# Two graph-attention layers on one core: three row-sum counts per sample instead of six, and five projections issued in halves

## The chip, the cores and the metric

The kernel runs on one core of a Trainium2 chip. The metric is the device time of one execution in microseconds (us). Before the change it is 3097.54 us, the median of three runs (3097.45 to 3101.15).

The engines named below are those of the profile: PE does the matrix multiplications (PEld is its weight load), DVE, ACT and POOL are the vector, scalar and general engines, and SP issues transfers (DMAs). Each engine works through its own queue in the order in which the program was written.

## The reference

Sixteen samples of 1024 nodes with 256 features go through two attention layers. What is computed, cut to what matters:

```
for layer in (0, 1):                      # 4 heads of 64, then 8 heads of 32
    h = relu(layernorm(x))                # per node
    q, k, v = h Wq, h Wk, h Wv            # layer 1 adds biases
    s = q k^T / sqrt(D), -inf where adj == 0
    x = x + (softmax(s) v) Wo + bo        # softmax over the 1024 keys
```

All of it is in float32. The softmax needs two things of each masked and exponentiated score tile p (keys on the partitions, queries along the row): the product with v, and the sum over the keys by which the product is divided.

## The kernel before, in words

**Steps.** The work of a layer on one sample is cut into groups: two halves of 512 queries (`qh`), and in each half two groups of heads (`g`). A group of layer 1 has four heads and eight steps; step j takes the 128 keys of tile j against 512 queries for all four heads. A group of layer 0 has four steps. A layer-0 sample is 16 steps, a layer-1 sample 32. The stream runs layer 0 of sample 0 and then, for b = 0, 1, ..., layer 0 of sample b+1 and layer 1 of sample b. In this document c is the first step of layer 1 of a sample b; its four groups start at c, c+8, c+16 and c+24, and c+32 begins the next layer-0 stage. A *pair* is an even step and the odd one behind it.

**What a step does.** `scores` (line 459) makes four products of 128 by 512, in two PSUM tiles of two banks each. `exponentials` lets DVE mask each tile into SBUF (line 482, two instructions) and ACT take the exponential in place (line 488). Two steps later, `weigh` (line 500) multiplies the exponentials with v. POOL then adds the odd step's tiles to the even step's (line 613).

**PSUM.** All tiles of two banks come from one pool with three buffers, handed out in turn (`psum_pair`): two for the scores of each step, and one for every projection (`kq` and `values`: q, k and v of another sample or layer) or output product (`end_half`). So without a projection the scores of the next step take the buffer that is left over and the first of this step; with one in between they take both buffers of this step, and must wait until DVE has read them.

**Where a projection goes.** The stream of `Stream.run` is written out by hand: `later(i, f)` puts f at step i. Functions in `LARGE` (k, q, values, end_half) are issued at the end of their step. If an even layer-1 step has one, its `weigh` is put off to the odd step, which then does two. PE's order in such a pair is: scores, projection, scores, weigh, weigh. In a pair without one it is scores, weigh, scores, weigh.

**The sums over keys.** `count` (line 351) multiplies exponentials with a matrix of ones. In layer 1 a tile is first added up on the way: POOL adds odd to even steps, and `accumulate` (line 597) is a DMA from POOL's queue that adds one even step's tile of 1 MB to another's. For groups 0 to 2 of a sample the tiles of steps 0 to 3 are added into one and counted, and those of steps 4 to 7 into another and counted: six counts in a sample, of which five are issued in two halves of 256 columns, in steps of their own (`halves`), and one whole (512 columns). Each is put at a fixed number of steps after its tile (`waits`). The last group has one count. After the count come `spread`, `invert`, `fetch` and `normalize`, at steps after the group's end that the tuple `at` gives. The sample before the last and the last sample have orders of their own for some groups (`brief`, `pairs`).

**The projections of the next layer-0 sample.** While layer 1 of sample b runs, `block_inputs` puts the k, q and v products of sample b+2's layer 0 into its steps: for the first half of the nodes at c+8 (k), c+16 (q) and c+18 (v), for the second at c+22 (k), c+26 (q) and c+30 (v). There are fourteen such samples (b = 0 to 13).

The exponentials' tiles of even steps have seven buffers, those of odd steps two (for each half): DVE in step j+4 writes where POOL's addition of step j read.

Of the kernel before, what the change touches and what calls it, by code (L numbers as in the profile page):

```python
# [18 lines left out]
P = 128  # L19
# [71 lines left out]
def fast_program(ctx, tc, a, w, loads, chk):  # L91
# [89 lines left out]
    class Inputs:  # L181
# [76 lines left out]

        def kq(self, half, is_q):
            if half == 0 and not is_q:  # L260
                self.kT = actp.tile([P, 2, N], F32, tag="kT", name=f"kT_{self.n}")
                self.v = actp.tile([P, NT, E], F32, tag="v", name=f"v_{self.n}")
            if is_q:
                to = self.qT[half] = actp.tile(
                    [P, 2, 512], F32, tag="qT", bufs=3, name=f"qT_{self.n}_{half}"
                )
            else:
                to = self.kT[:, :, ts(half, 512)]
            wt = w.q if is_q else w.k
            pq = psum_pair(f"pq_{self.n}_{half}_{int(is_q)}")  # L270
            for m in range(2):
                for c in range(2):
                    nc.tensor.matmul(  # L273
                        pq[:, m, :], wt[self.layer][:, c, ts(m, P)], self.hT[half][:, c, :],
                        start=(c == 0), stop=(c == 1),
                    )
            if self.layer == 0:
                if is_q:
                    nc.vector.tensor_copy(to, pq)
                else:  # L280
                    nc.scalar.copy(to, pq)
            else:
                for m in range(2):
# [14 lines left out]

        def k(self, half):
            self.kq(half, False)  # L300

        def q(self, half):
            self.kq(half, True)

        def values(self, half):
            pv = psum_pair(f"pv_{self.n}_{half}").rearrange("p a (t e) -> p (a t) e", e=E)
            for i in range(4):
                for c in range(2):
# [3 lines left out]
                    )  # L312
            nc.scalar.copy(self.v[:, ts(half, 4), :], pv)

# [4 lines left out]
    class Group:  # L319


        def __init__(self, inp, mask, qh, g, half):
# [10 lines left out]

            self.waits = ((5, 5), (7, 7), (7, 6), None)[2 * qh + g]

# [190 lines left out]
    class Stream:  # L526
# [72 lines left out]
        def count_steps(self, i, st):  # L599
# [7 lines left out]
            elif j % 2:  # L607
# [8 lines left out]
                elif gr.pairs:  # L616
                    self.halves(i + 3, gr, one, j == 1, False)
                elif j == 1:
                    gr.one = one
                elif j == 3:  # L620
                    self.accumulate(one, gr.one)
                    gr.one = one
                    if not gr.last:
                        self.halves(i + gr.waits[0], gr, one, True, False)
                    if gr.brief:
                        self.later(i + 6, gr.count, one, True, False)
                elif gr.brief and j == 5:
                    self.halves(i + 5, gr, one, False, False)
                elif gr.brief:
                    self.later(i + 4, gr.count, one, False, st.last)  # L630
                elif j == 5:
                    gr.two = one
# [21 lines left out]
        def end_group(self, i, gr):  # L654
# [121 lines left out]
    def block_inputs(inp, half, turn, put, place, *at):  # L776
# [4 lines left out]
        for i, f in zip(at, (inp.k, inp.q, inp.values)):  # L781
            later(i, f, half)

# [18 lines left out]
    for b in range(B - 1):  # L802
# [14 lines left out]
        if b + 2 < B:  # L817
# [3 lines left out]
            if b == 0:  # L821
                norms(other, 0, a + 12, a + 14, c, c + 1, bias=c + 34)
                block_inputs(other, 0, c + 2, c + 3, c + 4, c + 8, c + 16, c + 18)
                norms(other, 1, c + 3, c + 4, c + 6, c + 7, bias=c + 36)
                block_inputs(other, 1, c + 8, c + 9, c + 12, c + 22, c + 26, c + 30)
# [267 lines left out]
```

## Time and profile before

| | |
|---|---|
| median of three runs | 3097.54 us |
| the profiled execution's own time | 3100.21 us |
| its span, first to last instruction | 3098.4 us |
| PE busy | 3072.7 us, 99% of the span |
| DVE busy | 2484.3 us, 80% |
| POOL busy | 2352.5 us, 76% |
| ACT busy | 2233.5 us, 72% |
| accumulating DMAs (line 597) | 133, 7.8 us each from issue to landing, 920 ns of POOL for each issue |
| layer-1 stage of sample 5 (1151.43 to 1264.48 us) | 113.05 us: PE 113.02, DVE 94.80, POOL 94.60, ACT 82.83 busy |

The page's first part gives each engine's busy time and its share of the span. PE is busy nearly all the time, so time is gained or lost where PE gets less or more to do, or where it is made to wait. The samples repeat almost exactly: the distance from the layer-1 stage's start to the next layer-0 stage is 113.05 to 114.06 us in samples 1 to 13. So the steps of one sample, read from the timeline, stand for the others.

### The profile page before, as it was taken

What the parts mean: (1) busy time and instruction counts of PE and PEld (TensorE: products, weight loads), DVE (VectorE), ACT (ScalarE), POOL (GpSimd) and SP (SyncE); (2) the same over time, 40 slices, a digit from 0 to 9 for tenths busy, and PEclk for the clock granted to TensorE, in tenths of its full rate; (3) what the DMA queues carried; (4) which work ended last, traced back from release to release, by engine and by line L of the source; (5) the groups of instructions that cost most, each with busy time, mean ns of one, the idle gap of its engine ahead of it and who ended that gap; (6) DMA issues with size and microseconds to landing.
All of it is one profiled execution on the core that took longest, in us unless ns stands there. A gap on an engine that the chain in (4) does not pass through costs nothing.

```text
span 3098.4 us, 47101 instructions
## 1 busy us (share of the span) xinstructions
PE 3072.7 (99%) x17404; PEld 1221.5 (39%) x17404; DVE 2484.3 (80%) x2754; ACT 2233.5 (72%) x2440; POOL 2352.5 (76%) x1358
## 2 busy tenths in 40 slices
PE   9999999999999999999999999999999999999998
PEld 4443433434334343343434334343343433434332
DVE  5778788887878888788887888878788787887776
ACT  6677777777777777777777777777777777776775
POOL 3568778687887868778687786877868788786886
PEclk9999999999999999999999999999999999999999
DMA  4225546454453544635445463554545545453331
GB/s 129 59 64 118 127 105 130 121 109 119 108 136 111 117 118 104 143 108 117 121 102 135 107 129 106 114 130 106 127 115 111 127 109 122 118 114 85 76 77 33
DMA packets 259230, 341.38 MB, mean 110 GB/s; under 512 B 58288, under 2 KB 218288, under 8 KB 241968
## 3 DMA queue, kind: packets, MB, share of 16 engines
q0 software_dynamic: 19152, 139.47, 22.9%
q1 hardware_dynamic: 239840, 198.82, 22.7%
q8 instruction: 139, 2.28, 0.3%
q14 instruction: 99, 0.81, 0.1%
HBM read 149.95 MB, written 47.96 MB: 64 GB/s over the span
## 4 chain that ended last, share of the span: by engine, by line
PE 93%; DMA 2%; DVE 2%; ACT 1%; SPq 1%; POOL 1%; issue 1%; DVEq 0%; ACTq 0%; POOLq 0%
PE ps L459 31%; PE po L500 29%; PE pq L273 14%; PE pv L309 8%; PE py L441 7%; PE pz L351 4%; DMA turned<-hn 1%; DVE p L482 1%; POOL p L613 1%; SPq L152 0%; ACT p L488 0%; DMA inv<-vd 0%; DMA p<-p 0%; DMA sums<-s 0%; ACT hn L217 0%
## 5 line engine op out<-in xcount | busy, mean ns | idle before, releaser
L482 DVE SCALAR_TENSOR_TENSOR p<-mask,ps 128x1024 f32<-128x1024 fp8e5 x1536 | 1792.7, 1215 | 352.2 <-PE ps L459 337.2
L488 ACT ACTIVATE p<-p 128x1024 f32<-128x1024 f32 x1536 | 1607.2, 1056 | 630.9 <-DVE p L482 574.6
L613 POOL TENSOR_TENSOR p<-p,p 128x1024 f32<-128x1024 f32 x510 | 1212.5, 2428 | 170.7 <-PE po L500 170.7
L459 PE MATMUL ps<-qT,kT 32*128 32x512 f32 (+1 forms) x6144 | 1070.1, 628 | 4.5 <-DVE p L482 2.6
L500 PE MATMUL po<-p,v 128*32 128x512 f32 (+1 forms) x6144 | 980.9, 600 | 2.6 <-ACT cat L363 2.2
L459 PEld LDWEIGHTS ps<-qT,kT 32*128 32x128 f32 (+1 forms) x6144 | 348.9, 184 | 586.6 <-issue 248.5
L500 PEld LDWEIGHTS po<-p,v 128*32 128x32 f32 (+1 forms) x6144 | 234.5, 118 | 683.0 <-issue 480.9
L513 POOL TENSOR_TENSOR p<-p 128x1024 f32<-128x1024 f32 x128 | 302.4, 2363 | 134.8 <-DVE p L512 129.4
L512 POOL TENSOR_TENSOR p<-p,p 128x1024 f32<-128x1024 f32 x64 | 150.8, 2356 | 204.3 <-DVE p L509 188.3
L411 POOL TENSOR_TENSOR cat<-cat,inv 128x512 f32<-128x512 f32 x127 | 175.7, 1390 | 94.0 <-DMA inv<-vd 93.8
L309 PE MATMUL pv<-wv,hT 128*128 128x256 f32 x1024 | 237.8, 385 | 0.0
L441 PE MATMUL py<-wo,cat 128*128 128x256 f32 x1008 | 236.0, 387 | 1.5 <-POOL cat L411 1.5
L273 PE MATMUL pq<-hT,wq 128*128 128x512 f32 x512 | 236.6, 605 | 0.1
L273 PE MATMUL pq<-hT,wk 128*128 128x512 f32 x512 | 236.6, 605 | 0.1
L309 PEld LDWEIGHTS pv<-wv,hT 128*128 128x128 f32 x1024 | 189.4, 190 | 72.5 <-DVE p L482 21.4
L441 PEld LDWEIGHTS py<-wo,cat 128*128 128x128 f32 x1008 | 187.1, 191 | 76.7 <-issue 25.1
L351 PE MATMUL pz<-p,ones 128*32 128x256 f32 (+1 forms) x1928 | 181.3, 445 | 0.9 <-DMA p<-p 0.9
L509 DVE TENSOR_TENSOR p<-p 128x1024 f32<-128x1024 f32 x128 | 179.8, 1405 | 0.0
L597 POOL DMA_DIRECT2D p<-p x133 | 122.4, 920 | 63.3 <-POOL p L613 30.6
L217 ACT ACTIVATE hn<-x,shift,rstd 128x256 f32<-128x256 f32 x256 | 138.2, 588 | 43.6 <-DMA turned<-hn 29.3
L446 DVE TENSOR_TENSOR x<-py,x 128x1024 f32<-128x1024 f32 x63 | 77.1, 1224 | 102.0 <-PE py L441 101.3
L363 ACT COPY cat<-po 128x512 f32<-128x512 f32 x128 | 73.3, 573 | 116.6 <-PE py L441 96.5
(52 smaller groups left out, 1702.6 us busy)
## 6 DMA issues: line engine op xcount, KB each, us to landing
p<-p POOLq DMA_DIRECT2D x133, 1024.0 KB, 7.8
adj<-in_adj_dram SPq DMA_DIRECT2D x512, 128.0 KB, 3.1
turned<-hn SPq DMA_DIRECT2D x58, 512.0 KB, 3.8
hT<-turned SPq DMA_DIRECT2D x232, 128.0 KB, 2.9
x<-in_x_dram SPq DMA_DIRECT2D x128, 128.0 KB, 3.1
inv<-vd SPq DMA_DIRECT2D x128, 128.0 KB, 3.0
inv<-vd SPq DMA_DIRECT2D x252, 64.0 KB, 3.5
out_dram<-x SPq DMA_DIRECT2D x124, 128.0 KB, 2.2
```

The lines of the kernel that those rows point to most:

```text
L273: nc.tensor.matmul(pq[:, m, :], wt[self.layer][:, c, ts(m, P)], self.hT[half][:, c, :], start=(c == 0), stop=(c == 1),)
L309: nc.tensor.matmul(pv[:, i, :], self.hT[half][:, c, ts(i, P)], w.v[self.layer][:, c, :], start=(c == 0), stop=(c == 1),)
L351: nc.tensor.matmul(self.s[ts(r, 32), q], w.ones.to_broadcast([P, 32]), of[:, q], start=start and not part, stop=stop and part != 0,)
L411: nc.gpsimd.tensor_mul(o, o, inv)
L441: nc.tensor.matmul(py[:, i, :], self.half.cat[:, c, ts(i, P)], w.o[self.layer][:, c, :], start=(c == 0), stop=(c == 1),)
L459: nc.tensor.matmul(st.ps[i // 2][:, i % 2, :], gr.inp.kT[r * D : (r + 1) * D, gr.g, ts(kt, P)], gr.inp.qT[gr.qh][r * D : (r + 1) * D, gr.g ...
L482: nc.vector.scalar_tensor_tensor(out=half, in0=gr.mask.m[gr.qh][:, kt // 4, :, kt % 4].unsqueeze(1).to_broadcast([P, 2, 512]), scalar=-EDG ...
L488: nc.scalar.activation(half, half, AF.Exp, scale=gr.scale)
L500: nc.tensor.matmul(gr.o[r * D : (r + 1) * D, :], gr.inp.v[:, kt, h * D : (h + 1) * D], st.halves[i // 2][:, i % 2, :], start=(kt == 0), st ...
L509: nc.vector.tensor_add(a, a, b)
L513: nc.gpsimd.tensor_add(a, a, b)
L613: nc.gpsimd.tensor_add(half, half, of)
```

## The change

Groups 0, 1 and 2 of a layer-1 sample get one count instead of two. The tile of steps 0 and 1 is added by DMA to that of steps 2 and 3 as before; that one is now added to the tile of steps 4 and 5, and that to the tile of steps 6 and 7, two steps later. The three DMAs follow each other, since each reads what the one before wrote. The last tile is counted whole (512 columns), nine steps after the group's last addition (eight for the third group), and `spread` and `invert` move back to match; `normalize` and `end_half` keep their steps.

`k`, `q` and `values` take an argument `part`. With it they issue only one half of the products, into a PSUM tile of their own, and copy out only that half. Five of the six projections of sample b+2 are issued in this way, each half in an even step: k at c+8 and c+10, q at c+14 and c+16, and for the second half of the nodes k at c+20 and c+22, q at c+24 and c+26, v at c+28 and c+30. The first half's v stays whole at c+18.

```diff
-        def kq(self, half, is_q):
+        def kq(self, half, is_q, part=None):
...
-            pq = psum_pair(f"pq_{self.n}_{half}_{int(is_q)}")
-            for m in range(2):
+            pq = psum_pair(f"pq_{self.n}_{half}_{int(is_q)}_{part}")
+            parts = slice(0, 2) if part is None else slice(part, part + 1)
+            for m in range(2)[parts]:
...
             if self.layer == 0:
                 if is_q:
-                    nc.vector.tensor_copy(to, pq)
+                    nc.vector.tensor_copy(to[:, parts], pq[:, parts])
                 else:
-                    nc.scalar.copy(to, pq)
+                    nc.scalar.copy(to[:, parts], pq[:, parts])
...
-        def values(self, half):
-            pv = psum_pair(f"pv_{self.n}_{half}").rearrange("p a (t e) -> p (a t) e", e=E)
-            for i in range(4):
+        def values(self, half, part=None):
+            pv = psum_pair(f"pv_{self.n}_{half}_{part}").rearrange("p a (t e) -> p (a t) e", e=E)
+            tiles = slice(0, 4) if part is None else slice(2 * part, 2 * part + 2)
+            for i in range(4)[tiles]:
...
-            nc.scalar.copy(self.v[:, ts(half, 4), :], pv)
+            nc.scalar.copy(self.v[:, ts(half, 4), :][:, tiles], pv[:, tiles])
...
-            self.waits = ((5, 5), (7, 7), (7, 6), None)[2 * qh + g]
+            self.waits = (9, 9, 8, 4)[2 * qh + g]
...
-                elif j == 3:
-                    self.accumulate(one, gr.one)
-                    gr.one = one
-                    if not gr.last:
-                        self.halves(i + gr.waits[0], gr, one, True, False)
...
-                elif not gr.last:
-                    self.accumulate(one, gr.two)
-                    if gr.qh:
-                        self.later(i + 6, gr.count, one, False, True)
-                    else:
-                        self.halves(i + gr.waits[1], gr, one, False, True)
-                else:
-                    self.later(i + 1, self.accumulate, one, gr.two)
-                    self.later(i + 4, gr.count, one, True, True)
+                elif gr.last and j == 5:
+                    gr.two = one
+                elif not st.last:
+                    self.accumulate(one, gr.one)
+                    gr.one = one
+                else:
+                    of, k = (gr.two, 1) if gr.last else (gr.one, 2)
+                    self.later(i + k, self.accumulate, one, of)
+                    self.later(i + gr.waits, gr.count, one, True, True)
...
-                at = ((6, 12, 15, 19), (8, 12, 14, 17, 19), (6, 9, 11, 14), None)[2 * gr.qh + gr.g]
+                at = ((10, 13, 15, 19), (10, 14, 15, 18, 19), (8, 11, 12, 14), None)[2 * gr.qh + gr.g]
...
         for i, f in zip(at, (inp.k, inp.q, inp.values)):
-            later(i, f, half)
+            if type(i) is tuple:
+                for part in range(2):
+                    later(i[part], f, half, part)
+            else:
+                later(i, f, half)
...
-                block_inputs(other, 0, c, c + 1, c + 2, c + 8, c + 16, c + 18)
+                block_inputs(other, 0, c, c + 1, c + 2, (c + 8, c + 10), (c + 14, c + 16), c + 18)
...
-                block_inputs(other, 1, c + 7, c + 8, c + 12, c + 22, c + 26, c + 30)
+                block_inputs(other, 1, c + 7, c + 8, c + 12, (c + 20, c + 22), (c + 24, c + 26), (c + 28, c + 30))
```

More of the change, by code (lines that the diff above doesn't have):

```diff
@@ L257, in place_blocks @@
                 )
-        def kq(self, half, is_q):
-            if half == 0 and not is_q:
+        def kq(self, half, is_q, part=None):
+            if half == 0 and not is_q and not part:
                 self.kT = actp.tile([P, 2, N], F32, tag="kT", name=f"kT_{self.n}")
@@ L263, in kq @@
             if is_q:
-                to = self.qT[half] = actp.tile(
-                    [P, 2, 512], F32, tag="qT", bufs=3, name=f"qT_{self.n}_{half}"
-                )
+                if not part:
+                    self.qT[half] = actp.tile(
+                        [P, 2, 512], F32, tag="qT", bufs=3, name=f"qT_{self.n}_{half}"
+                    )
+                to = self.qT[half]
             else:
@@ L278, in kq @@
                 if is_q:
-                    nc.vector.tensor_copy(to, pq)
+                    nc.vector.tensor_copy(to[:, parts], pq[:, parts])
                 else:
-                    nc.scalar.copy(to, pq)
+                    nc.scalar.copy(to[:, parts], pq[:, parts])
             else:
-                for m in range(2):
+                for m in range(2)[parts]:
                     if is_q:
@@ L297, in test, with k, q @@
                 )
[L299 to L303, printed above, removed]
-        def values(self, half):
-            pv = psum_pair(f"pv_{self.n}_{half}").rearrange("p a (t e) -> p (a t) e", e=E)
-            for i in range(4):
+        def k(self, half, part=None):
+            self.kq(half, False, part)
+        def q(self, half, part=None):
+            self.kq(half, True, part)
+        def values(self, half, part=None):
+            pv = psum_pair(f"pv_{self.n}_{half}_{part}").rearrange("p a (t e) -> p (a t) e", e=E)
+            tiles = slice(0, 4) if part is None else slice(2 * part, 2 * part + 2)
+            for i in range(4)[tiles]:
                 for c in range(2):
@@ L619, in count_steps @@
                     gr.one = one
-                elif j == 3:
+                elif gr.brief:
+                    if j == 3:
+                        self.accumulate(one, gr.one)
+                        self.later(i + 6, gr.count, one, True, False)
+                    elif j == 5:
+                        self.halves(i + 5, gr, one, False, False)
+                    else:
+                        self.later(i + 4, gr.count, one, False, True)
+                elif gr.last and j == 5:
+                    gr.two = one
+                elif not st.last:
                     self.accumulate(one, gr.one)
                     gr.one = one
-                    if not gr.last:
-                        self.halves(i + gr.waits[0], gr, one, True, False)
[L625 to L632, printed above, removed]
-                elif not gr.last:
-                    self.accumulate(one, gr.two)
-                    if gr.qh:
-                        self.later(i + 6, gr.count, one, False, True)
-                    else:
-                        self.halves(i + gr.waits[1], gr, one, False, True)
-                else:
-                    self.later(i + 1, self.accumulate, one, gr.two)
-                    self.later(i + 4, gr.count, one, True, True)
+                else:
+                    of, k = (gr.two, 1) if gr.last else (gr.one, 2)
+                    self.later(i + k, self.accumulate, one, of)
+                    self.later(i + gr.waits, gr.count, one, True, True)
         def halves(self, i, gr, one, start, stop):
@@ L822, in fast_program @@
                 norms(other, 0, a + 12, a + 14, c, c + 1, bias=c + 34)
[L823 removed]
+                block_inputs(other, 0, c + 2, c + 3, c + 4, (c + 8, c + 10), (c + 14, c + 16), c + 18)
                 norms(other, 1, c + 3, c + 4, c + 6, c + 7, bias=c + 36)
[L825 removed]
+                block_inputs(other, 1, c + 8, c + 9, c + 12, (c + 20, c + 22), (c + 24, c + 26), (c + 28, c + 30))
             else:
                 norms(other, 0, a + 10, a + 12, a + 13, a + 15, bias=c + 34)
[L828 removed]
+                block_inputs(other, 0, c, c + 1, c + 2, (c + 8, c + 10), (c + 14, c + 16), c + 18)
                 norms(other, 1, c + 2, c + 4, c + 5, c + 6, bias=c + 36)
[L830 removed]
+                block_inputs(other, 1, c + 7, c + 8, c + 12, (c + 20, c + 22), (c + 24, c + 26), (c + 28, c + 30))
             at = 5, 8, 10, 12, 14, 45, 49, 51, 53
```

## The prediction

> **What bounds the kernel now.** First the page: engines and the chain that ended last.
>
> ```profile
> PE 3072.7 (99%) x17404; PEld 1221.5 (39%) x17404; DVE 2484.3 (80%) x2754; ACT 2233.5 (72%) x2440; POOL 2352.5 (76%) x1358
> ...
> PE 93%; DMA 2%; DVE 2%; ACT 1%; SPq 1%; POOL 1%; issue 1%; DVEq 0%; ACTq 0%; POOLq 0%
> ```
>
> PE is never idle for long and carries the chain. Second, the groups with the shapes apart: the counts and DVE's masking.
>
> ```profile
> L351 PE MATMUL pz<-p,ones 128*32 128x256 f32 x1360 | 107.0, 380 | 0.9 <-DMA p<-p 0.9
> L351 PE MATMUL pz<-p,ones 128*32 128x512 f32 x568 | 75.0, 600 | 0.0
> L597 POOL DMA_DIRECT2D p<-p x133 | 122.4, 920 | 63.3 <-POOL p L613 30.6 <-PE po L500 17.3 <-DMA p<-p 12.2
> ```
>
> By these rows fewer counts look like pure gain. Whether they are shows only in the order of time: PE's timeline in sample 5 (start, length, line), from step c+13 (1202.21).
>
> ```profile
> 1202.21 1.14 PE L459 MATMUL ps<-qT,kT 32*128 32x512 f32 x8
> 1203.28 1.92 PE L500 MATMUL po<-p,v 128*32 128x512 f32 x16
> 1205.14 1.14 PE L459 MATMUL ps<-qT,kT 32*128 32x512 f32 x8
> 1206.21 1.07 PE L500 MATMUL po<-p,v 128*32 128x512 f32 x8
> 1207.09 0.61 PE L351 MATMUL pz<-p,ones 128*32 128x256 f32 x8
> 1207.64 1.14 PE L459 MATMUL ps<-qT,kT 32*128 32x512 f32 x8
> ...
> 1210.13 1.15 PE L459 MATMUL ps<-qT,kT 32*128 32x512 f32 x8
> 1211.29 3.70 PE L273 MATMUL pq<-hT,wq 128*128 128x512 f32 x8
> 1214.92 0.71 PE L459 MATMUL ps<-qT,kT 32*128 32x512 f32 x4
> ```
>
> DVE's timeline beside it, and its place at step c+8, whose scores start at 1184.70:
>
> ```profile
> 1206.31 2.35 DVE L482 SCALAR_TENSOR_TENSOR p<-mask,ps 128x1024 f32<-128x1024 fp8e5 x2 [0.51 <-PE ps L459]
> 1208.88 4.78 DVE L482 SCALAR_TENSOR_TENSOR p<-mask,ps 128x1024 f32<-128x1024 fp8e5 x4 [0.22 <-PE ps L459]
> ...
> 1185.47 1.24 DVE L243 STREAM_TRANSPOSE hn<-hn 128x1024 f32<-128x1024 f32 x1
> 1186.63 2.31 DVE L482 SCALAR_TENSOR_TENSOR p<-mask,ps 128x1024 f32<-128x1024 fp8e5 x2
> ```
>
> Read three things. A step with half a count lasts 2.50 us (1205.14 to 1207.64), and DVE's two maskings take 2.39 of it. From the start of the scores DVE needs 1.17 us to begin and is done with both tiles at 1208.66, 3.52 to 3.53 us after. A whole projection puts the odd step's scores 4.79 us behind the even step's (1210.13 to 1214.92): 1.16 of scores, 3.63 of products. So today they never meet a tile that DVE still reads. Where they do, in sample 14, the trace shows what happens:
>
> ```profile
> 2886.53 1.13 PE L459 MATMUL ps<-qT,kT 32*128 32x512 f32 x4
> 2886.91 6.81 DVE L482 SCALAR_TENSOR_TENSOR p<-mask,ps 128x1024 f32<-128x1024 fp8e5 x6
> 2888.12 1.13 PE L459 MATMUL ps<-qT,kT 32*128 32x512 f32 x4 [0.47 <-DVE p L482]
> 2889.18 1.07 PE L500 MATMUL po<-p,v 128*32 128x512 f32 x8
> ```
>
> The first tile's products run, the second tile's wait for the end of a masking, and the step's weigh starts 1.06 us after they begin, so the whole delay passes on.
>
> **The change part by part. Counts.** A sample loses ten half counts and one whole, and gains three whole ones. By PE's rows a half adds 0.43 us to a step (2.50 against 2.07 us for a bare step of sample 14, 2884.46 to 2886.53), a whole one 0.86 behind weighs (step c+31 lasts 3.78 against 2.92) or 1.00 between scores and a projection (c+4 lasts 5.72, c+2 4.72). But the steps with half counts are at another limit: the next step's second tile needs the buffer whose masking ends 2.46 us after the scores' start, so a removed half gives back 0.04 of its 0.43. That gain must come from filling the room with the halved projections.
>
> **Halved projections.** The same products in twice as many tiles. A half is 1.8 to 1.9 us of PE, so the odd step's scores could start 3.0 us after the even step's. They take the two buffers of those scores, as the projection has the third; the second is free at 3.53. Then come 1.06 us to the weighs and 1.86 us of two weighs (1203.28 to 1205.14): a pair lasts 3.53 + 1.06 + 1.86 = 6.45 us, where PE alone would need 3.0 + 2.92 = 5.92. Behind the waiting scores stand both weighs and the next scores on PE; DVE, ACT and POOL wait for these.
>
> Now the twelve pairs from c+8 to c+30. Before, by the starts of the scores: 7.63, 5.08, 7.73, 5.00, 7.71, 7.65, 5.00, 7.71, 5.00, 7.71, 5.00, 8.58, together 79.8 us (1184.70 to 1264.48). After:
> - c+10, 14, 16, 20, 22, 28, 30: 6.45 each.
> - c+8: DVE comes late from the transposition at c+7 and ends 4.24 us after the scores (1186.63 + 2.31 - 1184.70): 4.24 + 2.92 = 7.16.
> - c+12, an output product: 7.73 as before. c+18: 7.65 + 1.00 for the first group's count = 8.65. c+26: count and half projection, 1.07 + 1.0 + 1.9 + 2.92 = 6.9; the count covers the wait.
> - After c+16: DVE does statistics until 4.76 us after the scores, then the q copy (0.61, half of the 1224 ns row, to 0.75, the row of the same size with a bias; I take 0.65), so its next masking ends at 6.6 and c+18 loses 0.15.
> - After c+22: transposition and statistics end at 5.88 in the trace, the reciprocal moved here (0.25) makes it 6.1, the next masking ends at 7.25 and the one behind at 8.4. The scores of c+24 wait until 7.25, its own maskings run from 8.4 to 10.7, and the pair ends at 10.7 + 2.92 = 13.6 instead of 12.9: c+24 counts 7.19.
>
> Together 82.9 us: +3.1. The third group's count lands at c+33, in layer 0, where PE is the limit: +0.86. So +4.0 us a sample; fourteen samples: +56 us. Sample 14 has the new counts without halves; its POOL-bound pair at c+14 (13.19 us) may gain or lose. I take 0, between -3 and +4.
>
> **The rest, costed at nothing.** 45 more accumulating DMAs are 45 x 0.92 = 41 us of POOL, which has 94.6 of 113 us of work in the stage; a pair with one is 4.72 + 0.92 = 5.64 of 6.45. The second DMA of a group waits for the first: issued a pair apart, with 7.8 us from issue to landing, it holds POOL's queue 1.35 us, and the statistics' small operations and the next additions stand behind it. DVE wants the second half of an odd tile some 0.7 us after POOL frees it. In the first group the pair is 7.63 long; in the second the pair behind is c+18, with its whole v; in the third c+26 has the count. I take 0; the other end is DVE 1.5 us late in two groups of each sample, +42. Each count stands at least three pairs behind its last DMA's issue, and all seven even buffers come free before reuse. ACT gets three copies in halves (2 x 0.57 for 1.01), DVE two: 0.1 us each, in idle time. On SP the four small DMAs of `spread` move to c+19, c+27 and c+33; behind the last stands a mask load that is used a layer-0 pair (9 us) later and lands in 3.1, so that is free.
>
> The profiled execution took 3100.2 us, so this sum gives 3156; against the median of the runs, 2.7 lower, 3154.
>
> **Two rules beside the trace.** The Trainium skill (Perfetto Trace Analysis, section Optimization Strategy) says that the same gap repeating on the engine that should be saturated can mean too little PSUM for the next tile. The 0.47 us row above is such a gap, and a projection in halves asks for one more tile each; by this rule the sum is the one above, and by PE's work alone it would be 3065. The same skill (DMA: Bandwidth & Descriptors, section Anatomy of one DMA — SWDGE (gpsimd) path) fits a POOL-issued DMA with 2.0 us + bytes / 436e3, which is an estimated 4.4 us for 1 MB; the trace has 7.8, and goes into the sum. By the page no DMA would wait for another.
>
> **The rivals.** *The fill works (ends on the other side).* If DVE freed the second tile by 3.0 us, nine pairs would last 5.92, and 53.3 + 7.73 + 8.65 + 6.9 = 76.6, +0.86 = -2.4 us a sample: 3065. For it: PE sat idle only 1.3 us in all of the run for DVE's masking before the layer-1 scores (the scores' row by shape). Against: the 3.53 repeats at nearly every step. It decides where half a projection takes more than 2.4 us or masking ends 0.5 us sooner. *The late maskings are absorbed:* without the three extra terms (0.7, 0.15, 0.74), +2.4 a sample: 3131. *POOL becomes the wait:* DVE stands behind additions held by the serial DMA, +42: 3196; the point is POOL starting a pair's additions over 0.7 us behind the weighs. For it: in sample 14 POOL already held DVE for 1.66 us at 2909.26. *The counts do not pay at all* is part of the forecast.
>
> **How the numbers follow.** Forecast 0.62, absorbed 0.12, POOL 0.14, fill works 0.08; 0.04 for something between fill and absorbed. 0.2% of the time is 6 us, about what a measurement tells from no change. Slower: 0.62 + 0.12 + 0.14 + 0.02 = 0.90, same 0.02, faster 0.08. The range leaves out the fill, the cases between, and some of the POOL case: 3128 to 3195.
>
> **What would show it.** In the timeline after, pairs with half a projection last 6.4 to 6.5 us from scores to scores; in the odd step the second tile's products begin 3.53 us after the even step's scores, on the end of a masking, so that these scores' merged row lengthens from 1.14 to some 1.6 us. PE's idle time hardly grows by the page, since the first tile's products fill most of the wait: the loss shows in the pairs, not in the share. Masking still follows the scores by 1.17 us. Wrong if those pairs last 5.9, if POOL's additions appear as DVE's releaser in most samples, or if the layer-0 stages lengthen by more than the count.

## The result, and the profile after

The changed kernel takes 3198.16 us, the median of four runs (3192.42 to 3200.18); the kernel before, on the same chip, 3098.58. The ratio is 1.032 (95% interval 1.0305 to 1.0331): slower by about 100 us, where 56 had been forecast. The direction held, and so did the reason for the part that lies in layer 1; the time lies 3 us above the range. Below, the numbers behind a time are its ratio to the kernel before, run beside it, and the 95% interval. Each time is the median of the executions in the faster of two states; one execution of experiment 8, 3495.73 us at a granted clock of 0.849 where the others have 0.994 to 0.996, is left out.

The page after, engines, then the row of POOL's issues of the accumulating DMAs.

```profile
PE 3139.8 (98%) x16444; PEld 1228.5 (38%) x16444; DVE 2522.4 (79%) x2782; ACT 2249.1 (70%) x2482; POOL 2387.7 (75%) x1403
```

```profile
L601 POOL DMA_DIRECT2D p<-p x178 | 163.2, 917 | 136.2 <-DMA p<-p 102.4
```

The groups with the shapes apart, of the changed kernel: layer 1's scores and the counts (columns: count of instructions, busy us, mean ns, idle time before them and what ended it).

```profile
L463 PE MATMUL ps<-qT,kT 32*128 32x512 f32 x4096 | 682.1, 641 | 6.4 <-DVE p L486 3.3 <-ACT kT L290 1.6
L355 PE MATMUL pz<-p,ones 128*32 128x512 f32 x808 | 106.9, 601 | 0.0
L355 PE MATMUL pz<-p,ones 128*32 128x256 f32 x160 | 12.4, 381 | 0.0
```

The work did get less: the counts take 119.3 us where they took 182.0. Yet PE is "busy" 67 us longer. Layer 1's scores alone went from 592.3 to 682.1 us with the same 4096 instructions and nearly the same mean (640 and 641 ns). A step's scores are two tiles side by side; where the second waits, the first covers it, and the page books the wait as busy time. PE's timeline of sample 5 shows it, from c+14 (1238.28):

```profile
1238.28 1.14 PE L463 MATMUL ps<-qT,kT 32*128 32x512 f32 x8
1239.35 1.98 PE L276 MATMUL pq<-hT,wq 128*128 128x512 f32 x4
1241.26 1.72 PE L463 MATMUL ps<-qT,kT 32*128 32x512 f32 x8
1242.91 1.92 PE L504 MATMUL po<-p,v 128*32 128x512 f32 x16
1244.77 1.14 PE L463 MATMUL ps<-qT,kT 32*128 32x512 f32 x8
```

DVE's timeline beside it:

```profile
1239.45 2.35 DVE L486 SCALAR_TENSOR_TENSOR p<-mask,ps 128x1024 f32<-128x1024 fp8e5 x2 [0.50 <-PE ps L463]
1241.72 0.68 DVE L282 COPY qT<-pq 128x512 f32<-128x512 f32 x1
```

The odd step's scores begin 2.98 us after the even step's and last 1.72 us instead of 1.14, because their second tile waits for DVE, which is done with the even step's second tile only at 1241.80 (1239.45 + 2.35), 3.52 us after its scores. The pair lasts 6.49 us (1238.28 to 1244.77); 6.45 was forecast, 5.92 is PE's work.

From the first to the last scores the run got 97.1 us longer (3049.3 to 3146.4, by the starts of the scores). They come from these places, to the rounding:

| place | before | after | forecast of the difference |
|---|---|---|---|
| layer-1 pairs of fourteen samples | 113.30 a sample | 116.51, together +44.9 | +44 (14 x 3.15) |
| c+32, the third group's count | 9.12 | 9.98, together +12.0 | +12 |
| c+40, a layer-0 pair | 11.05 | 13.16, together +29.5 | 0 |
| the other layer-0 pairs | 56.36 | 56.57, together +3.0 | 0 |
| sample 14's layer 1 | 114.00 | 114.72, +0.7 | 0 (-3 to +4) |
| the last sample | 100.78 | 107.79, +7.0 | 0 |

So the layer-1 stage costs what the forecast said. What was missed lies outside it, above all at c+40. The timelines of SP, DVE and PE in sample 5 around it (c+36 starts at 1320.70, c+40 at 1339.91), after:

```profile
1334.51 2.49 SPq L152 DMA_DIRECT2D adj<-in_adj_dram  x4
1337.05 2.54 SPq L407 DMA_DIRECT2D inv<-vd  x4
1339.69 2.66 SPq L388 DMA_DIRECT2D sums<-s  x4
```

```profile
1344.01 0.25 DVE L396 RECIPROCAL vn<-sums 128x16 f32<-128x16 f32 x1 [3.65 <-DMA sums<-s]
1344.18 4.55 DVE L486 SCALAR_TENSOR_TENSOR p<-mask,ps 128x1024 f32<-128x1024 fp8e5 x4
```

```profile
1345.39 1.56 PE L463 MATMUL ps<-qT,kT 64*128 64x512 f32 x4 [2.64 <-DVE p L486]
1346.88 4.87 PE L504 MATMUL po<-p,v 128*64 128x512 f32 x16
```

and the same place of SP and PE before (c+36 starts at 1284.45, c+40 at 1303.66):

```profile
1287.59 2.24 SPq L403 DMA_DIRECT2D inv<-vd  x4
1298.20 2.76 SPq L152 DMA_DIRECT2D adj<-in_adj_dram  x4
1301.07 3.01 SPq L384 DMA_DIRECT2D sums<-s  x4
```

```profile
1306.74 1.13 PE L459 MATMUL ps<-qT,kT 64*128 64x512 f32 x4 [0.23 <-DVE p L482]
1307.80 3.65 PE L500 MATMUL po<-p,v 128*64 128x512 f32 x16
```

The third group's `fetch` (four DMAs, 2.54 us of SP) stood at c+36 before the change and stands at c+37 now: the third entry of its tuple `at` went from 11 to 12. The last group's `spread` is at c+37 as well, and so is a mask load (line 152), which SP issues 13.8 us after the scores of c+36 in both kernels. Before, the fetch went out ahead of that load, and SP then stood until 1298.20 in any case. Now the fetch has to wait behind the load, between it and the four small DMAs with the last group's sums. These are issued 19.0 us after the scores of c+36 instead of 16.6; DVE's reciprocal stands 3.65 us at the head of DVE's queue waiting for them, and four maskings stand behind it. PE waits 2.64 us where it waited 0.23. Then comes something more: the weigh behind the wait takes 4.87 us, not 3.65. The table by stretches of the changed kernel (stretch; its length and PE's busy time, PEld, DVE, ACT and POOL; then PE's granted clock, DMA share, GB/s) says why:

```profile
1346.00:1348.00 2.00, 2.00 (x8) 0.50 (x6) 2.00 (x3) 1.86 (x3) 0.19 (x1) 0.50 0.74 277
1348.00:1350.00 2.00, 2.00 (x9) 0.53 (x8) 1.97 (x4) 1.86 (x3) 0.00 (x0) 0.66 0.78 212
1350.00:1352.00 2.00, 2.00 (x11) 0.59 (x8) 1.48 (x2) 1.11 (x2) 0.31 (x1) 1.00 0.71 201
```

After the gap the granted clock falls to half for some three microseconds. The pair went from 11.37 to 15.43 us: 2.41 of waiting, 0.43 and 1.22 of the same products at half rate. Samples 3 to 6 had this (14.7 to 15.4 us); nine others took 12.5 to 12.7 us (10.9 to 11.9 before), and sample 13 lost nothing.

The row for that reciprocal sums the waits over the run: 38.3 us now against 15.4 before.

```profile
L396 DVE RECIPROCAL vn<-sums 128x16 f32<-128x16 f32 x95 | 22.9, 241 | 38.3 <-DMA sums<-s 37.9
```

### The profile page after: what moved, and what is told of

Same layout as the page of the kernel before. It is cut to its first block, busy times and chain, and to the rows that moved or that the text cites. A ratio compares the mean times of both kernels' runs of the same rounds, so it can differ in the third digit from the quotient of the medians.

```text
span 3196.3 us, 45453 instructions
## 1 busy us (share of the span) xinstructions
PE 3139.8 (98%) x16444; PEld 1228.5 (38%) x16444; DVE 2522.4 (79%) x2782; ACT 2249.1 (70%) x2482; POOL 2387.7 (75%) x1403
## 5 line engine op out<-in xcount | busy, mean ns | idle before, releaser
L617 POOL TENSOR_TENSOR p<-p,p 128x1024 f32<-128x1024 f32 x510 | 1215.3, 2449 | 171.1 <-PE po L504 166.3
L463 PE MATMUL ps<-qT,kT 32*128 32x512 f32 (+1 forms) x6144 | 1165.7, 630 | 31.1 <-DVE p L486 25.1
L463 PEld LDWEIGHTS ps<-qT,kT 32*128 32x128 f32 (+1 forms) x6144 | 388.1, 184 | 721.1 <-DVE p L486 307.4
L516 POOL TENSOR_TENSOR p<-p,p 128x1024 f32<-128x1024 f32 x64 | 150.8, 2356 | 184.0 <-DVE p L513 169.0
L601 POOL DMA_DIRECT2D p<-p x178 | 163.2, 917 | 136.2 <-DMA p<-p 102.4
L513 DVE TENSOR_TENSOR p<-p 128x1024 f32<-128x1024 f32 x128 | 215.1, 1681 | 0.4 <-issue 0.2
L313 PE MATMUL pv_None<-wv,hT 128*128 128x256 f32 x800 | 185.7, 385 | 0.0
L313 PEld LDWEIGHTS pv_None<-wv,hT 128*128 128x128 f32 x800 | 148.0, 190 | 57.2 <-issue 34.1
L167 ACT ACTIVATE mask<-adj,numbers 128x1024 fp8e5<-128x1024 int32 x128 | 145.7, 1140 | 30.9 <-DMA adj<-in_adj_dram 30.9
L217 ACT ACTIVATE hn<-x,shift,rstd 128x256 f32<-128x256 f32 x256 | 138.1, 588 | 29.1 <-DMA turned<-hn 18.3
L226 POOL TENSOR_TENSOR x<-x,bo 128x1024 f32<-128x1024 f32 x64 | 156.8, 2522 | 0.0
L519 POOL TENSOR_TENSOR p<-p,p 128x1024 f32<-128x1024 f32 x64 | 151.7, 2370 | 5.0
L178 ACT ACTIVATE mask<-mask,numbers 128x1024 fp8e5<-128x1024 fp8e5 x128 | 144.1, 1136 | 0.0
```

Source lines behind the costliest of these rows:

```text
L226: nc.gpsimd.tensor_add(rows, rows, w.bo[self.layer].unsqueeze(1).to_broadcast([P, 4, E]))
L313: nc.tensor.matmul(pv[:, i, :], self.hT[half][:, c, ts(i, P)], w.v[self.layer][:, c, :], start=(c == 0), stop=(c == 1),)
L463: nc.tensor.matmul(st.ps[i // 2][:, i % 2, :], gr.inp.kT[r * D : (r + 1) * D, gr.g, ts(kt, P)], gr.inp.qT[gr.qh][r * D : (r + 1) * D, gr.g ...
L513: nc.vector.tensor_add(a, a, b)
L601: nc.gpsimd.dma_start(one, two, accum_op=ALU.add)
L617: nc.gpsimd.tensor_add(half, half, of)
```

## The experiments

All kernels here compute the whole reference; they differ in order, buffers and the way of the sums alone.

**1. The counts alone**, with all projections whole at their old steps.

```diff
-                block_inputs(other, 0, c, c + 1, c + 2, (c + 8, c + 10), (c + 14, c + 16), c + 18)
+                block_inputs(other, 0, c, c + 1, c + 2, c + 8, c + 16, c + 18)
...
-                block_inputs(other, 1, c + 7, c + 8, c + 12, (c + 20, c + 22), (c + 24, c + 26), (c + 28, c + 30))
+                block_inputs(other, 1, c + 7, c + 8, c + 12, c + 22, c + 26, c + 30)
```

> The changed kernel with whole projections at their old steps, so only the counts and the serial DMAs are changed. Theory A (two losses: in layer 1 the halved projections make the odd step's scores wait for PSUM buffers, about 45 us; in layer 0 a late transfer of the last group's sums holds DVE, about 30 us of the 45 there): the layer-1 stage falls below that of before, since pairs that lost their half counts go from 5.00 to 4.5 us as in sample 14 (five pairs, -2.5), and whole counts at c+18 and c+26 cost 1.0 each and the one at c+30 goes (-0.9): -1.4 us a sample; the layer-0 stages keep all of their +3.2 us a sample and the end its +8 us: about 3098 - 19 + 45 + 8 = 3131. Rival B (the serial DMAs hold POOL and POOL holds DVE in layer 1): the layer-1 stages stay 3 us longer than before and the time stays near 3198.

Measured: 3179.89 us, 1.0262 (1.0245 to 1.0279), between the two expectations. The layer-0 stages are 3.25 us longer, as the expectation had it (c+40 is late here too, 12.85), and the last sample 5.3 (8 was expected). The bare pairs came out at 4.50 as expected as well. The miss is the rest of layer 1, which is 1.8 us a sample longer where 1.4 shorter was expected: c+12 lasts 9.35 us, not 7.7, c+24 5.53, not 4.5, and c+16, c+22 and c+30 7.9, some 0.2 more than expected. For c+12 the timelines show the POOL rival of the prediction at work. In sample 5, POOL at the second DMA of the group, then DVE and PE at c+12:

```profile
1216.24 0.88 POOL L601 DMA_DIRECT2D p<-p  x1 [1.05 <-DMA p<-p]
1216.85 2.83 POOL L415 TENSOR_TENSOR cat<-cat,inv 128x512 f32<-128x512 f32 x2
1219.35 7.32 POOL L617 TENSOR_TENSOR p<-p,p 128x1024 f32<-128x1024 f32 x3
```

```profile
1224.38 3.48 DVE L486 SCALAR_TENSOR_TENSOR p<-mask,ps 128x1024 f32<-128x1024 fp8e5 x3 [0.96 <-POOL p L617]
```

```profile
1225.65 3.72 PE L445 MATMUL py<-wo,cat 128*128 128x256 f32 x16 [1.06 <-DVE p L486]
```

POOL stands 1.05 us for the first DMA before it can issue the second; normalisation and additions follow late, DVE's masking waits 0.96 us for an addition, PE's output product 1.06 us for a buffer that DVE holds. So without the halves POOL does become the wait; with them the pairs are long enough (6.49 us) that c+12 lasts 7.84.

**2. The halves alone**, with the counts, their DMAs and the times of the kernel before.

```diff
-            self.waits = (9, 9, 8, 4)[2 * qh + g]
+            self.waits = ((5, 5), (7, 7), (7, 6), None)[2 * qh + g]
...
-                at = ((10, 13, 15, 19), (10, 14, 15, 18, 19), (8, 11, 12, 14), None)[2 * gr.qh + gr.g]
+                at = ((6, 12, 15, 19), (8, 12, 14, 17, 19), (6, 9, 11, 14), None)[2 * gr.qh + gr.g]
```

Between the two places `count_steps` has its old branches back.

> The kernel before with its counts, and only the five projections in halves at the new steps. Theory A: pairs without a count 6.5 us (the wait for the buffers), pairs that keep their half counts about 6.9 us (the half count between scores and projection covers the wait, and costs its own time), c+8 7.2, c+30 7.4; together 84.2 us for the twelve pairs against 79.8: +4.4 us a sample in layer 1, nothing in layer 0: about 3160. The DMA transfers and POOL's queue are those of before, so rival B (the serial DMAs) expects about 3098, or less.

Measured: 3161.40 us, 1.0203 (1.0186 to 1.022), as the theory of the buffers had it. Pairs with half a projection last 6.49, with a half count beside it 6.93; layer 1 takes 117.88 us a sample against 113.30, layer 0 is unchanged (76.56 against 76.53), and so is the last sample (100.78). The halves alone cost 62 us, all in layer 1; the counts alone 81; both together 100, not 143. The difference lies in layer 1, where the halves alone cost 4.6 us a sample, the counts alone 1.8 and both together 3.2: the longer pairs hide waits that the counts alone bring, c+12 above all.

**3. The fetch a step later.** The changed kernel with one number changed: the third group's `fetch` goes behind the last group's sums in SP's queue.

```diff
-                at = ((10, 13, 15, 19), (10, 14, 15, 18, 19), (8, 11, 12, 14), None)[2 * gr.qh + gr.g]
+                at = ((10, 13, 15, 19), (10, 14, 15, 18, 19), (8, 11, 13, 14), None)[2 * gr.qh + gr.g]
```

> The changed kernel with one number moved: the third group's fetch one step later (12 to 13), so that its four DMAs stand behind the last group's four sums DMAs in SP's queue and not ahead of them. Theory A: the sums land 2 us earlier, DVE's reciprocal at c+39 waits 0.5 us as before instead of 2.6 to 3.2, the layer-0 pair at c+40 goes back from 13.2 (mean) to about 11.0 us: 14 x 2.1 = 29 us less, about 3169. Rival C (a third more bytes of accumulating DMA slow the small transfers): the pair keeps its length, 3198.

Measured: 3170.31 us, 1.0226 (1.0209 to 1.0243): 28 us of the 100 hang on this one place in a queue. (The fetch at its old step c+36, with the later `invert`, was not run.) c+40 goes from 13.16 to 10.94. In sample 5 the sums are now issued first, and the reciprocal waits 0.76 us:

```profile
1327.04 2.90 SPq L388 DMA_DIRECT2D sums<-s  x4
...
1336.24 1.82 SPq L407 DMA_DIRECT2D inv<-vd  x4
```

```profile
1331.11 0.26 DVE L396 RECIPROCAL vn<-sums 128x16 f32<-128x16 f32 x1 [0.76 <-DMA sums<-s]
```

**4. The weigh between.** Even steps with half a projection keep their weigh, so that PE does scores, weigh, half projection, scores, weigh, and the odd step's scores begin later.

```diff
-                f.__name__ in LARGE for f, _ in self.due.get(i, [])
+                f.__name__ in LARGE and len(args) < 2 for f, args in self.due.get(i, [])
```

> The changed kernel, but an even step with half a projection keeps its own weigh between its scores and the half projection (PE: scores, weigh, half, scores, weigh). All work, buffers and DMAs are the same, only PE's order differs. Theory A: the odd step's scores come 3.9 us after the even step's, when both tiles have been read (3.53): the pairs at c+10, 14, 16, 20, 28 and 30 go from 6.49 to 6.0 us, c+8 from 7.2 to 6.3, c+22 and c+24 together lose 0.4: 4.0 us a sample, about 3198 - 56 = 3142. If the half pairs are held by DVE, ACT or POOL instead, they keep 6.49 us and the time 3198.

Measured: 3209.69 us, 1.0362 (1.0344 to 1.0379): a miss. PE's timeline, sample 5, c+14 to c+17:

```profile
1244.70 1.98 PE L276 MATMUL pq<-hT,wq 128*128 128x512 f32 x4
1246.62 1.14 PE L463 MATMUL ps<-qT,kT 32*128 32x512 f32 x8
1247.69 1.06 PE L504 MATMUL po<-p,v 128*32 128x512 f32 x8
1248.68 1.58 PE L463 MATMUL ps<-qT,kT 32*128 32x512 f32 x8
```

The wait inside the pair is gone: the odd step's scores last 1.14 again, and c+14 and c+20 take 6.05 as expected. But the next even step's scores now come only 2.06 us behind the odd step's (1246.62 to 1248.68) and wait there for the masking (1.58 instead of 1.14). The pair behind such a pair therefore still takes 6.5 (c+16, 22, 28, 30: 6.49 to 6.51). The distance between scores that DVE needs was only moved across the boundary of the pair. Three other pairs got longer than in the changed kernel, c+12 8.39 (7.84), c+18 9.11 (8.65) and c+26 8.03 (6.91); what holds these was not looked into.

**5. The halves in another buffer.** The same products at the same steps, but the half projections (all but the second half of q at c+26) go to the one-bank buffer of the counts instead of the scores' rotation.

```diff
-            pq = psum_pair(f"pq_{self.n}_{half}_{int(is_q)}_{part}")
+            if part is None or (is_q and half == 1 and part == 1):
+                pq = psum_pair(f"pq_{self.n}_{half}_{int(is_q)}_{part}")
...
+            else:
+                pq = ps_o.tile([P, 512], F32, tag="pz", name=f"pq_{self.n}_{half}_{int(is_q)}_{part}")
```

> The changed kernel, whose halved projections (all but the second half of q at c+26) write into the one-bank buffer of the counts and not into a pair of banks of the rotation that the scores use. Products, steps, counts, DMAs: all as in the changed kernel. Theory A (the half projections lengthen the pairs because they take a buffer out of the scores' rotation, so the odd step's second tile waits for a masking that ends 3.53 us after the even step's scores): now the odd step needs only the first tile's masking (ends 2.4 us after), and the pairs go to PE's own work, 5.9 to 6.0: c+10, 14, 16, 20, 28, 30 from 6.49 to 6.0, c+8 from 7.2 to 6.0, c+22 and c+24 together 0.4 shorter; -4.6 us a sample, x14 = -64: about 3134 us; up to 3160 if additions behind the serial accumulating DMAs hold DVE's masking in the first or second group as soon as the pairs are shorter. Rival B (the 6.49 is the price of DVE's, ACT's or POOL's work in halves, not of the buffer): pairs stay at 6.4 to 6.5, 3198 us. The layer-0 stages keep c+40's 13.2 in either case.

Measured: 3218.94 us, 1.0382 (1.0366 to 1.0398), slower than the changed kernel. For the pairs the theory holds: c+10, 14, 16 and 22 last 5.91, c+30 5.92, c+8 6.07 (5.9 to 6.0 was expected), and the odd step's scores last 1.14 again. So it is the buffer, not the work in halves, that costs 0.58 us a pair. The sum did not hold, since the shorter pairs brought new waits: c+12 9.74 (7.84), c+18 9.24 (8.65), c+20 8.92 (6.49), c+28 7.33 (6.49). POOL and PE of sample 5:

```profile
1229.91 0.89 POOL L612 DMA_DIRECT2D p<-p  x1 [1.19 <-DMA p<-p]
```

```profile
1239.28 3.72 PE L456 MATMUL py<-wo,cat 128*128 128x256 f32 x16 [1.19 <-DVE p L497]
...
1270.18 2.66 PE L283 MATMUL pq<-hT,wk 128*128 128x512 f32 x4 [2.13 <-ACT s L386]
```

The first two rows are the wait of experiment 1 at c+12. The third is a conflict that the edit itself made: at c+20 the half projection takes the bank that the count of c+18 has just filled, and waits 2.13 us until ACT has copied it out; at c+28 the same with the count of c+26.

**6. The DMAs of a group apart**, in the kernel of experiment 1: the second DMA a pair later, the third at i + 4.

```diff
-                elif gr.last and j == 5:
+                elif j == 5:
                     gr.two = one
-                elif not st.last:
+                elif j == 3:
...
-                    of, k = (gr.two, 1) if gr.last else (gr.one, 2)
-                    self.later(i + k, self.accumulate, one, of)
+                    if not gr.last:
+                        self.accumulate(gr.two, gr.one)
+                    self.later(i + (1 if gr.last else 4), self.accumulate, one, gr.two)
```

> The kernel of the counts alone, with a group's second accumulating DMA (pair 4 into pair 2) issued a pair later, behind its fourth pair's additions, and the third one two steps after its old place, so that no DMA is issued while the one before it has not landed. Counts at the same steps; the same arithmetic. Theory (in the kernel of the counts alone, c+12 lasted 9.35 against 7.73 because POOL stands at the second DMA's issue for the first, and with it the additions that DVE's masking needs): c+12 back to 7.7 to 7.9, c+24 from 5.53 to 4.5 to 5.0, POOL's waits at the DMA issues for DMA p<-p from 119 to under 30 us; 2 us a sample, 3180 - 28 = about 3150 us. Rival (the 1.6 us at c+12 come from the bare pairs before it: DVE simply has more masking waiting): times as before, 3180 us, with c+12 over 9.

Measured: 3416.73 us, 1.1023 (1.1006 to 1.104). What the theory names came as expected: c+12 7.92, c+24 4.50, POOL's waits for DMAs 18.3 us. But the third DMA now meets the next group's first in POOL's queue. POOL, then PE, in sample 5:

```profile
1307.09 1.75 POOL L601 DMA_DIRECT2D p<-p  x2 [0.30 <-POOL p L617]
```

```profile
1319.18 1.23 PE L355 MATMUL pz<-p,ones 128*32 128x512 f32 x8 [2.94 <-DMA p<-p]
1320.34 5.20 PE L313 MATMUL pv_None<-wv,hT 128*128 128x256 f32 x16
```

The two were issued together from 1307.09 on. By their landings in the trace the first, the next group's, is there at 1314.09, the second, the third of its group, only at 1319.05, 12 us behind, where the median DMA lands in 7.9; the count that needs the second starts at 1319.18. The counts at c+18, c+26 and c+32 wait for DMAs 183.4 us over the run, and the product behind each wait is slow as well (5.20 us for 3.72). The count's distance of nine steps had no 5 us to spare.

**7. Everything together**: experiment 5's buffers, experiment 6's DMAs, experiment 3's fetch, and sample 14's counts as before the change.

```diff
-                at = ((10, 13, 15, 19), (10, 14, 15, 18, 19), (8, 11, 12, 14), None)[2 * gr.qh + gr.g]
+                at = ((10, 13, 15, 19), (10, 14, 15, 18, 19), (8, 11, 13, 14), None)[2 * gr.qh + gr.g]
+                if gr.old:
+                    at = ((6, 12, 15, 19), (8, 12, 14, 17, 19), (6, 9, 11, 14))[2 * gr.qh + gr.g]
```

> All findings together: the changed kernel with its half projections in the counts' bank, a group's accumulating DMAs a pair apart, the third group's fetch a step later, and sample 14's counts and times as in the kernel before. Sum by the theory: layer 1's sixteen pairs 113.3 + 3.2 - 4.6 = 111.9 us a sample, layer 0 76.5 + 0.9 = 77.4: -0.5 us a sample against before, x14 = -7, sample 14 and the last sample as before: 3092 us, between 3080 and 3110. If the buffers are not what costs the halves, about 3150; if POOL's additions hold DVE in the shorter pairs, 3110 to 3130.

Measured: 3424.65 us, 1.1042 (1.1027 to 1.1057): experiment 6's waits rule it (c+18 15.08, c+32 18.43). What it does tell: c+40 is back at 11.00, and the last sample takes 100.78 us exactly as before, where it takes 107.76 in experiment 5. Sample 14's counts at their old places account for the +7.0; the other changes leave the last sample late (108.32 in experiment 3, 107.76 in 5, 106.15 in 8).

**8. The third DMA a step sooner** than in experiment 6.

```diff
-                    self.later(i + (1 if gr.last else 4), self.accumulate, one, gr.two)
+                    self.later(i + (1 if gr.last else 3), self.accumulate, one, gr.two)
```

> The kernel of the counts alone with the second accumulating DMA of a group behind its fourth pair's additions, and the third three steps later, a step before the next group's first DMA comes due: each of the four is issued a pair apart from its neighbours. In the run before (third DMA four steps later) POOL issued the third together with the next group's first DMA, the two shared the engines and landed after 12 to 14 us, and the counts at c+18, c+26 and c+32 waited for them. Theory (the 1.6 us at c+12 and the 1.1 at c+26 of the counts alone are POOL held by a DMA that waits for the one before): c+12 7.7 to 7.9, c+24 4.5 to 5.0, c+26 8.7 to 8.9, c+18 8.65, no count waits for a DMA; layer 1 112.8 us a sample where the counts alone had 115.1: 3180 - 33 = about 3147 us. c+40 stays late (12.9 us), since the fetch stands where it stood. Rival (the distance does not matter, the counts wait anyway or POOL is held elsewhere): 3180 us or more.

Measured: 3179.99 us, 1.0268 (1.0248 to 1.0289), no gain over experiment 1. No count waits any more, and c+12 lasts 7.92: for c+12 the theory holds. c+24 (5.43) and c+26 (8.89) stay as in experiment 1. At c+24 it is not POOL that is late but again a reciprocal at the head of DVE's queue, in experiment 1 (2.31 us) as here, as DVE's row of sample 5 shows (c+24 starts at 1262.91); the eight maskings behind it run without a gap to 1272.5:

```profile
1263.24 0.25 DVE L396 RECIPROCAL vn<-sums 128x16 f32<-128x16 f32 x1 [2.32 <-DMA sums<-s]
1263.41 9.13 DVE L486 SCALAR_TENSOR_TENSOR p<-mask,ps 128x1024 f32<-128x1024 fp8e5 x8
```

And the gain is given back: c+16 8.56 (7.90 in experiment 1), c+32 10.41 (9.98), c+34 12.26 (11.44). POOL's waits for DMAs fell only from 119.4 to 69.3 us: at c+33 of sample 5 the last group's second DMA still waits 5.21 us for its first (4.71 in experiment 1).

**9. What the runs would keep**: experiment 8's DMAs, halves only for the first half's k and q, in the counts' bank, the later fetch, and sample 14 as before.

```diff
-                block_inputs(other, 1, c + 7, c + 8, c + 12, (c + 20, c + 22), (c + 24, c + 26), (c + 28, c + 30))
+                block_inputs(other, 1, c + 7, c + 8, c + 12, c + 22, c + 26, c + 30)
```

> What the runs so far would keep of the change: the new counts with their DMAs a pair apart as in the run beside this one; halves for two projections only, k at c+8 and c+10 and q at c+14 and c+16, in the counts' bank; the other three projections whole at c+22, c+26 and c+30; the third group's fetch a step later; sample 14 as in the kernel before. Sum from pairs that were seen: 6.07, 5.91, 7.70, 5.91, 5.91, 8.65, 4.50, 7.91, 4.6, 8.8, 4.50, 7.92, together 78.4 against 79.8 before; +0.86 for the count at c+32: -0.5 us a sample, -8 in all: about 3091 us, 3080 to 3110. If POOL's DMAs hold DVE in the shorter pairs (c+12 at 9.7, c+18 at 9.2 as in the run with the counts' bank), 3120 to 3130.

Measured: 3139.01 us, 1.0133 (1.0116 to 1.015): the best of the kernels with the new counts, and still 1.3% above the kernel before. Layer 1 is at last no slower (113.16 us a sample against 113.30; c+18 9.31 where 8.65 was expected, c+24 5.36 where 4.6 was), and the last sample is at 100.78. What remains is layer 0: c+32 10.32 and c+34 12.43 against 9.12 and 10.85. In sample 5 the last group's second DMA is issued 10.5 us after the scores of c+32 (1278.92) instead of 5.1, and PE's scores at c+35 wait for ACT's copy of k. POOL, ACT and PE:

```profile
1289.47 0.88 POOL L614 DMA_DIRECT2D p<-p  x1 [6.21 <-PE pq_None L283]
```

```profile
1289.38 1.15 ACT L167 ACTIVATE mask<-adj,numbers 128x1024 fp8e5<-128x1024 int32 x1 [2.07 <-DMA adj<-in_adj_dram]
...
1290.90 1.27 ACT L297 ACTIVATE kT<-pq_None,bk 128x512 f32<-128x512 f32 x2
```

```profile
1292.22 1.99 PE L476 MATMUL ps<-qT,kT 64*128 64x512 f32 x8 [1.33 <-ACT kT L297]
```

The profile puts POOL's wait down to the k product of the next sample, whose result this DMA doesn't touch. The landings in the trace say what it was. The last group's first DMA, issued at 1277.64 while the third group's last was under way (1271.78 to 1280.30), lands only at 1288.93, and POOL goes on 0.54 us later; in experiments 1 and 8 it goes on just as long after the same landing, and there the profile names the DMA. A mask load issued beside these DMAs (its last part at 1278.45) lands at 1289.27, after 10.8 us where the median is 3.1. ACT waits 2.07 us for that, its copy of k stands behind, and PE waits for the copy. Over the run the layer-0 scores wait 17.0 us for k in this way, 14.9 in experiment 8 and not at all before. So the third group's last DMA came to lie on the last group's first; no run moved it away again. No version here beats the kernel before.

## Why the prediction was right and wrong

**Halved projections, right.** Seven pairs at 6.45 came out at 6.49; c+8 7.16 (7.16), c+18 8.65 (8.80, of which the 0.15 for a late masking did not come), c+24 7.21 (7.19), c+26 6.91 (6.9), c+12 7.84 (7.73). The sum for layer 1, 3.1 us a sample, measured 3.2. The cause, two buffers taken and the second free only 3.53 us after the even step's scores, is shown by experiment 5, where the same work in another bank gives 5.91. The rival "the fill works" is out, and so, but for that 0.15, is "the late maskings are absorbed".

**Counts, half right.** The three whole counts cost what was said (c+18 +1.00, c+32 +0.86). "A removed half gives back 0.04 of its 0.43" is wrong by size: where pairs are bare, in experiment 1, they last 4.50 instead of 5.00 us, 0.25 a step. The step of 2.46 us counts DVE's 1.17 us of beginning each time; once DVE is behind, its maskings follow each other, eight in 9.13 us (experiment 8), which is 2.28 for the two of a step. The changed kernel has no bare pair, so by luck its time did not suffer from that.

**POOL and the serial DMAs, right for this kernel only.** The rows after show POOL waiting 102.4 us for DMAs (12.2 before). In sample 5 these are 1.17 and 1.32 us at the second DMAs of the first two groups, where 1.35 was forecast, and the long pairs hide them (c+12 7.84 for 7.73). The larger part the prediction did not have: at c+33 the last group's second DMA waits for its first.

```profile
1308.46 0.87 POOL L601 DMA_DIRECT2D p<-p  x1 [4.51 <-DMA p<-p]
```

It costs little here: c+34, the pair behind it, accounts for nearly all of the +3.0 of the other layer-0 pairs (11.06 for 10.85); that this is the cause was not tried. The rival's mechanism is real: with shorter pairs it decided c+12 in experiments 1 and 5.

**The step that failed** is the sentence on SP: "behind the last stands a mask load that is used a layer-0 pair (9 us) later and lands in 3.1, so that is free". It looked at `spread`, at what stands behind it, and at the durations. It did not follow `fetch`. The text on the change does not name it either: besides `spread` and `invert`, the tuples `at` move the second group's `fetch` (14 to 15) and `normalize` (17 to 18) and the third group's `fetch` (11 to 12) by a step. The third group's four DMAs, which before went out ahead of a mask load that holds SP until 13.8 us after the scores of c+36, now come behind it, and the last group's sums behind them. Experiment 3 prices that place: 28 us, by the pair c+40 29.5. With it the sum of the prediction would have been 3154 + 29 = 3183, inside its range. The prediction had named the sign to look for, layer-0 stages longer by more than the count, and that is what the traces show. The sum for layer 1, its cause and the direction were right for the reason given; the term that SP's queue adds was put at nothing.

**Sample 14 and the rest.** "I take 0, between -3 and +4" for sample 14 holds for its own stage (+0.7), but its counts also delay the first pairs of the last sample, by 7.0 us (experiments 7 and 9 have 100.78 without them). The third pair takes 11.91 us for 9.51. In the first, 12.23 us for 7.63, POOL's issue and normalisation come ahead of its additions, DVE waits 0.50 and 1.10 us for these, PE's scores stretch to 1.92 us, PE then waits 1.20 us, the clock falls to 0.57, and k takes 5.40 us for 3.70. PE's timeline and the stretch behind it, after:

```profile
3062.78 1.92 PE L463 MATMUL ps<-qT,kT 32*128 32x512 f32 x8
3065.91 5.40 PE L276 MATMUL pq_None<-hT,wk 128*128 128x512 f32 x8 [1.20 <-DVE p L486]
```

```profile
3066.00:3070.00 4.00, 4.00 (x6) 1.70 (x7) 2.22 (x3) 3.06 (x3) 4.00 (x2) 0.57 0.97 197
```

The forecast thus lacked 29.5 + 7.0 + 3.0 + 0.7 = 40 of the 44 us by which it fell short, and 28 of these are the place of one fetch.

## What to carry to other kernels

Splitting an operation to fill gaps pays only if the halves don't ask for buffers of the rotation that the neighbours use: ask first what each new piece takes, and when that comes free. When steps move, list every issue of every moved function, in each queue, and see whom it now stands behind and ahead of; four small transfers that fell behind a held mask load, in front of another group's sums, cost more than a quarter of the loss here. And an engine's busy share can hide waits: read the distances between starts, not the share.

## What the runs showed of the hardware

**A wait on PE costs more than its length.** After a gap of 2.64 us (sample 5, c+40) the clock fell to 0.50 and 0.66 for two stretches of 2 us; after one of 2.13 us (experiment 5, c+20) to 0.84 and 0.50, and the product behind it took 2.66 us for 1.98. After 1.49 us (the same place in sample 9) nothing of the kind was seen. Over all eleven traces, without the start and the last 15 us, the granted clock fell to 0.50 within 4.5 us of the end of 5 of 94 gaps of 1.2 to 1.8 us, of 49 of 90 between 1.8 and 3 us, and of 66 of 68 over 3 us. The Trainium skill (TensorE: Matmul & The Clock Gate, section HAM oscillation — how this bites in real kernels) gives the rule as no idle gaps over some 3.4 us; here 2.1 to 2.6 us were enough in the cases shown, and about half of all gaps between 1.8 and 3 us, so a gap well under that length is not safe in this kernel.

**An addition on DVE stands still while POOL adds or multiplies beside it, or the other way round.** The layer-0 addition of one form (line 513, 509 before) rose from a mean of 1405 to 1681 ns with no change to it:

```profile
L513 DVE TENSOR_TENSOR p<-p 128x1024 f32<-128x1024 f32 x128 | 215.1, 1681 | 0.4 <-issue 0.2 <-PE po L504 0.2
```

In the changed kernel 97 of the 128 take 1.15 to 1.23 us. The other 31 are longer, up to 4.56 us, and each of these lies beside POOL's addition of the bias (line 226) or its normalisation (line 415). In sample 5:

```profile
1315.56 4.19 DVE L513 TENSOR_TENSOR p<-p 128x1024 f32<-128x1024 f32 x1
1313.70 4.97 POOL L226 TENSOR_TENSOR x<-x,bo 128x1024 f32<-128x1024 f32 x2
```

The two run beside each other for 3.11 us (1315.56 to 1318.67), and 4.19 less 3.11 is 1.08. All 31 come out at 1.08 to 1.10 us once the time beside POOL is taken off. Once, at 2897.81, it is the other way: the addition takes 1.15 us, all of it beside the bias addition, and that takes 3.43 us, where its median is 2.40. In experiment 6, where POOL does these operations at other times, 123 of the 128 are short and the mean is 1222 ns. No run was made to test this by itself.
